# Layer norms' inverse square root: a first guess from the exponent and three Newton steps on VectorE, in place of ScalarE's root

## The chip, the core and the metric

The kernel runs on one core of a Trainium2 chip. The metric is the device time of one execution in microseconds. A core has five engines, each with its own in-order instruction queue: TensorE (PE in the profile: matrix products), VectorE (DVE: elementwise work and reductions), ScalarE (ACT: functions from tables, copies), GpSimd (POOL: here mostly the issue of gathers) and SyncE (SP: the issue of plain DMAs). An instruction that waits holds up everything behind it in its queue.

## The reference, cut to what matters

Four layers run over 4096 nodes with 128 features and one 4096 x 4096 adjacency matrix that is mostly zero. Every layer begins with the same normalisation, and the last layer has a further one inside:

```python
def _layernorm(x, axis=-1, eps=1e-5):
    m = jnp.mean(x, axis=axis, keepdims=True)
    v = jnp.var(x, axis=axis, keepdims=True)
    return (x - m) / jnp.sqrt(v + eps)

# layer 0: neigh = adj @ h; x @ W_self.T + neigh @ W_neigh.T + b
# layer 1: out = h @ w[0] + (L @ h) @ w[1] + (2 L @ (L @ h) - h) @ w[2] + b
# layer 2: attention over the entries of adj, softmax by exp(max(0.2 C, C))
# layer 3: messages gelu(s_i + d_j + b) weighted by adj, an update, gelu, a layer norm with ln_w, ln_b
for layer in (0, 1, 2, 3):
    h = jnp.maximum(_layernorm(x, axis=-1), 0.0)
    x = x + layer_ref[layer](h, adj)
```

## The kernel before

The nodes stand in 32 blocks of 128 (a block is the partition dimension), handled in 8 groups of 4 blocks. The stages are:

- The adjacency matrix is read once, row block by row block. `mark` (L763) turns each half row block into a mask with ScalarE's Sigmoid, `scan` (L774) works on the mask with VectorE, and from it come lists of the non-empty parts (`row_flags`, `col_flags`, `pairs`).
- Three propagations (`Layer.load`, `Layer.gather`, `Layer.multiply`): dense tiles near the hub nodes come by plain DMA, rows for the listed parts by gathers that GpSimd issues (L553). `begin` (L967), `finish_0` (L985), `finish_1` and `finish_2` (L1019) follow a group's sums. Meanwhile `entries` (L806) decodes single matrix entries for the last layer.
- The attention (`Attention.attend`, L1216): Relu and Exp on ScalarE (L1229, L1232), two products on VectorE (L1236, L1238), two matmuls per tile (L1253, L1255). `finish_3` (L1268) closes a stripe.
- The messages (`Messages`, L1317): `prepare` (L1355) and `message` (L1394) use Gelu (L1377, L1415), `finish` (L1428) makes the update with a Gelu (L1444), the last norm, and writes the output.

The norms are in two places. `norm` (L557) is called by `begin` for 8 blocks at a time (4 calls), and by `finish_0`, `finish_2` and `finish_3` for 4 blocks (8 calls each): 28 calls. The last norm is written out in `Messages.finish` (L1445 to L1464), 8 times. Each one goes: a sum over the features on VectorE (L563, L1448) and its scaling to minus the mean (L564, L1449); one Square with a running sum per block on ScalarE (L568, L1453); the root on ScalarE (L572, L1456); the reciprocal on VectorE (L574, L1458) and minus mean times it (L575, L1459); then one Relu or Identity per block on ScalarE with the two as scale and bias (L578, L1462).

The order of the instructions on each engine isn't written out by hand. Every piece of work is a generator that yields what it needs next: an engine with an estimated time, a free buffer or an event. `Plan.run` (L299) simulates the engines while the program is built and gives the engine to the piece that can begin first, with ranks deciding among those that can begin within 0.3 us. A yield may carry the name of a function table; if it differs from the last one, the plan adds `TABLE = 1.3` us to ScalarE's time (L340). Plain matmuls on zeros fill gaps of TensorE (`fill`, L604). `in_order` (L348) then fixes the order found. So an edit to the estimates, or to the list of steps, changes the order everywhere after it.

If a capacity of the lists was exceeded, a dense version of the stack runs (`dense_stack`); with this data it doesn't run. It keeps its own norms.

Of the kernel before, what the change touches and what calls it, by code (L numbers as in the profile page):

```python
# [18 lines left out]
I32 = mybir.dt.int32  # L19
AF = mybir.ActivationFunctionType  # L20
ALU = mybir.AluOpType
# [5 lines left out]
D = 128  # L27
P = 128
# [3 lines left out]
GB = BANK // D  # L32
HALF = N // 2
QUARTER = N // 4
EPS = 1e-5
# [322 lines left out]
def on_dve(n):  # L358
    return "DVE", 0.16 + 1.05e-3 * n
# [7 lines left out]
def on_act(n, table=None):  # L367
    return ("ACT", 0.22 + 0.83e-3 * n) + ((table,) if table else ())
# [10 lines left out]
def sparse_stack(tc, x, adj, adjT, diag, w_self, w_neigh, b0, w1, b1, w2, att_src, att_dst,  # L379
# [7 lines left out]
    nc = tc.nc  # L387
    plan = Plan()
    EARLY = 7
    with ExitStack() as ctx:  # L390
# [7 lines left out]
        def kept(name, shape, dtype=F32):  # L398
            return keep.tile(list(shape), dtype, name=name, tag=name)
# [12 lines left out]
        def by_block(v, n):  # L412

            return v[:, None, :].to_broadcast([P, n, D])
# [31 lines left out]
        nc.gpsimd.memset(ones, 1.0)  # L446
        ones8 = kept("ones8", (P, 1), F8)
        nc.gpsimd.memset(ones8, 1.0)
        eps = kept("eps", (P, 1))
        nc.gpsimd.memset(eps, EPS)  # L450

        def iota(name, shape, pattern, base=0, step=0, dtype=F32):
            t = kept(name, shape, dtype)
# [100 lines left out]
                                         in_offset=bass.IndirectOffsetOnAxis(ap=index, axis=0))  # L554


        def norm(blocks, dst):  # L557

            n = blocks.stop - blocks.start
            st = yield stats  # L560
            src = xN[:, blocks, :]
            yield on_dve(n * D)
            nc.vector.tensor_reduce(st[:, 0, :n], src, axis=AX.X, op=ALU.add)  # L563
            nc.vector.tensor_scalar_mul(st[:, 0, :n], st[:, 0, :n], -1.0 / D)  # L564
            junk = yield junks
            yield "ACT", 0.58 * n
            for k in range(n):
                nc.scalar.activation(junk, src[:, k, :], AF.Square, bias=st[:, 0, k:k + 1],  # L568
                                     accum_out=st[:, 1, k:k + 1])
            plan.release(junks, junk)  # L570
            yield on_act(n, "sqrt")
            nc.scalar.activation(st[:, 1, :n], st[:, 1, :n], AF.Sqrt, bias=eps, scale=1.0 / D)  # L572
            yield "DVE", 0.35
            nc.vector.reciprocal(st[:, 2, :n], st[:, 1, :n])  # L574
            nc.vector.tensor_mul(st[:, 3, :n], st[:, 0, :n], st[:, 2, :n])  # L575
            yield "ACT", 0.45 * n
            for k in range(n):
                nc.scalar.activation(dst[:, k, :], src[:, k, :], AF.Relu, scale=st[:, 2, k:k + 1],  # L578
                                     bias=st[:, 3, k:k + 1])
            plan.release(stats, st)  # L580
# [12 lines left out]
        def times(p, n, terms):  # L593

            for k in range(n):
                for i, (lhs, w) in enumerate(terms):
                    nc.tensor.matmul(p[:, k * D:(k + 1) * D], lhs[:, k * P:(k + 1) * P], w, start=i == 0,  # L597
                                     stop=i == len(terms) - 1)
# [13 lines left out]
        def rows_of(p, n=GB):  # L612
            return p[:, :n * D].rearrange("p (k d) -> p k d", d=D)
# [353 lines left out]
        def begin(g):  # L967
            yield x_here[g]
            yield x_here[g + 1]
            blocks = slice(g * GB, (g + 2) * GB)  # L970
            yield from norm(blocks, hA[:, blocks, :])
            for k in range(2):
                h_done[g + k].set(plan.finish)
            yield SP
            nc.sync.dma_start(rows_in(h_tabs[0])[:, blocks, :], hA[:, blocks, :])
            landed = plan.transfer(2 * P * BANK * 4)
            for k in range(2):
                h0_table.set(landed)
            yield "POOL", 2.5
            nc.gpsimd.tensor_add(xN[:, blocks, :], xN[:, blocks, :], by_block(b0_sb, 2 * GB))  # L980
            for k in range(2):
                blocks = slice((g + k) * GB, (g + k + 1) * GB)
                yield from to_features(blocks, hA[:, blocks, :])

        def finish_0(g, agg):  # L985
            blocks = slice(g * GB, (g + 1) * GB)
            rows = xN[:, blocks, :]
            p = yield banks
            yield "PE", 8 * 0.42
            times(p, GB, [(hT[:, g * BANK:(g + 1) * BANK], w_self_sb), (agg, w_neigh_sb)])  # L990
            plan.release(aggs, agg)
            yield on_dve(BANK)
            nc.vector.tensor_add(rows, rows, rows_of(p))
            plan.release(banks, p)
            yield from norm(blocks, hB[:, blocks, :D])
            h1_done[g].set(plan.finish)
            yield SP
            nc.sync.dma_start(rows_in(h_tabs[1])[:, blocks, :], hB[:, blocks, :D])
            h1_table.set(plan.transfer(P * BANK * 4))
            yield "POOL", 1.4  # L1000
            nc.gpsimd.tensor_add(rows, rows, by_block(b1_sb, GB))
            yield from to_features(blocks, hB[:, blocks, :D])
# [16 lines left out]
        def finish_2(g, agg):  # L1019
# [9 lines left out]
            plan.release(banks, p)  # L1029
            h = yield h2s  # L1030
            yield from norm(blocks, h)
            yield from to_features(blocks, h)
            plan.release(h2s, h)
# [283 lines left out]
        class Messages:  # L1317
# [110 lines left out]
            def finish(self, g):  # L1428
                blocks = slice(g * GB, (g + 1) * GB)
                plan.release(s_tiles, self.s_rows[g])  # L1430
                agg = yield aggs
                yield on_act(BANK)
                nc.scalar.copy(agg, self.acc[g])
                plan.release(accs if g else picks, self.acc[g])
                p = yield banks
                yield "PE", 8 * 0.42
                times(p, GB, [(hT[:, g * BANK:(g + 1) * BANK], upd_h_sb), (agg, upd_a_sb)])
                plan.release(aggs, agg)
                f = yield f_tiles
                yield on_dve(BANK)  # L1440
                nc.vector.tensor_tensor(f, rows_of(p), by_block(upd_b_sb, GB), op=ALU.add)
                plan.release(banks, p)
                yield on_act(BANK, "gelu")
                nc.scalar.activation(f, f, AF.Gelu)  # L1444
                st = yield stats  # L1445
                yield "DVE", 1.5
                nc.vector.tensor_add(f, f, hA[:, blocks, :])
                nc.vector.tensor_reduce(st[:, 0, :GB], f, axis=AX.X, op=ALU.add)  # L1448
                nc.vector.tensor_scalar_mul(st[:, 0, :GB], st[:, 0, :GB], -1.0 / D)  # L1449
                junk = yield junks  # L1450
                yield "ACT", 0.58 * GB
                for k in range(GB):
                    nc.scalar.activation(junk, f[:, k, :], AF.Square, bias=st[:, 0, k:k + 1], accum_out=st[:, 1, k:k + 1])  # L1453
                plan.release(junks, junk)
                yield on_act(GB, "sqrt")
                nc.scalar.activation(st[:, 1, :GB], st[:, 1, :GB], AF.Sqrt, bias=eps, scale=1.0 / D)  # L1456
                yield "DVE", 0.35
                nc.vector.reciprocal(st[:, 2, :GB], st[:, 1, :GB])  # L1458
                nc.vector.tensor_mul(st[:, 3, :GB], st[:, 0, :GB], st[:, 2, :GB])  # L1459
                yield "ACT", 0.45 * GB  # L1460
                for k in range(GB):
                    nc.scalar.activation(f[:, k, :], f[:, k, :], AF.Identity, scale=st[:, 2, k:k + 1],  # L1462
                                         bias=st[:, 3, k:k + 1])
                plan.release(stats, st)  # L1464
                yield "DVE", 1.4
                nc.vector.tensor_mul(f, f, by_block(ln_w_sb, GB))
                nc.vector.tensor_add(f, f, xN[:, blocks, :])
                yield SP
                nc.sync.dma_start(out_rows[:, blocks, :], f)
                plan.release(f_tiles, f, plan.transfer(P * BANK * 4) - 1)  # L1470
                self.through.set(plan.finish)
# [115 lines left out]
        for i in range(2):  # L1587
# [6 lines left out]
            n = max(sum(u.cap for u in g.units) for g in GROUPS)  # L1594
# [67 lines left out]
def gnn_stack_kernel(tc, **args):  # L1662


    some_bad = sparse_stack(tc, **args)
    with tc.If(some_bad > 0):
        args.pop("diag")
        dense_stack(tc, **args)
# [329 lines left out]
```

## Time and profile before

| | us |
|---|---|
| median of 3 runs | 1176.93 |
| lowest and highest | 1172.99, 1178.95 |
| the profiled execution, its own time | 1485.49 |
| its span, first to last instruction | 1483.4 |

The profiled execution is 308.56 us longer than the median. The profile's rows of single instructions are the durations in that execution. TensorE's mean granted clock in it was 0.842 of full speed.

| engine | busy us | share of the span | instructions |
|---|---|---|---|
| PE | 1055.1 | 71% | 5943 |
| DVE | 792.7 | 53% | 2982 |
| ACT | 671.2 | 45% | 1344 |
| POOL | 766.4 | 52% | 832 |

A busy share is a mean over stages that differ: the reading of the matrix ends at about 340 us, the first three layers at about 900, the attention at about 1190, and the messages fill the rest. ScalarE's ACT_TABLE_LOAD rows are the changes of its function table; the row's line is that of the function that needed the new table.

### The profile page before, as it was taken

The page shows a single profiled execution, that of the slowest core. Times are in us where ns is not written, and L with a number is a line of the kernel's source. Part 1 is how long each engine was busy: PE and PEld are TensorE (multiplying, and loading weights), DVE is VectorE, ACT ScalarE, POOL GpSimd, SP SyncE. Part 2 cuts the span into 40 slices and gives each one's busy share as a digit, 9 for nine tenths or more (in the row PEclk, how much of TensorE's full clock was granted, in tenths as well). Part 3 has the DMA queues.
Part 4 walks back from the last instruction along what each step waited for, and adds up shares of the span by engine and source line. Part 5 has one row for each costly group of instructions (what it writes and reads, how often), then busy time and mean ns, then how long its engine had stood idle before and what let it go on. Part 6 is the DMA issues. An engine that isn't in the chain of part 4 may idle for free.

```text
span 1483.4 us, 19188 instructions
## 1 busy us (share of the span) xinstructions
PE 1055.1 (71%) x5943; PEld 722.2 (49%) x5943; DVE 792.7 (53%) x2982; ACT 671.2 (45%) x1344; POOL 766.4 (52%) x832
## 2 busy tenths in 40 slices
PE   6786778877486687667677069968767872957774
PEld 2454556554265465455555045534434452645663
DVE  5796567787466476345645048444444451424453
ACT  5983466664021213113335048656555630334366
POOL 4136664344635565546656733765557346664530
PEclk9897799897697899778888579979888995988988
DMA  8999899895565777766544034333333212112210
GB/s 252 357 329 334 286 299 330 305 353 185 135 185 147 211 228 227 201 187 181 150 115 132 8 93 132 107 88 89 88 107 97 61 50 49 42 42 53 61 45 24
DMA packets 175415, 236.03 MB, mean 159 GB/s; under 512 B 22452, under 2 KB 155336, under 8 KB 167112
## 3 DMA queue, kind: packets, MB, share of 16 engines
q1 hardware_dynamic: 148904, 186.45, 37.8%
q0 software_dynamic: 26400, 48.27, 13.6%
q8 instruction: 49, 0.80, 0.2%
q14 instruction: 62, 0.51, 0.1%
HBM read 203.41 MB, written 31.23 MB: 158 GB/s over the span
## 4 chain that ended last, share of the span: by engine, by line
PE 23%; another core or an unknown queue 13%; ACT 10%; DVE 7%; issue 6%; DMA 1%; POOL 0%; ACTq 0%; SPq 0%; DVEq 0%; POOLq 0%
PE acc L1253 4%; PE acc L1255 3%; PE bank L597 2%; PE acc L1421 2%; PE acc L1139 2%; PE acc L1156 2%; ACT junk L1453 1%; ACT e L1229 1%; ACT junk L568 1%; PE bank L1411 1%; PE pick L610 1%; ACT e L1232 1%; PE bank L1409 1%; DVE ehit L891 1%
## 5 line engine op out<-in xcount | busy, mean ns | idle before, releaser
L553 POOL DMA_INDIRECT e_val<-in_adj,e_at x158 | 154.5, 978 | 48.0 <-issue 45.6
L553 POOL DMA_INDIRECT g<-h_tab,fetch_row x136 | 136.1, 1001 | 73.0 <-issue 34.3
L610 PE MATMUL pick<-nothing 128*128 128x512 f16 x536 | 142.9, 416 | 1.6 <-issue 1.6
L1139 PE MATMUL acc<-big,hA 128*128 128x256 f32 x448 | 131.7, 442 | 10.7 <-issue 7.7
L610 PEld LDWEIGHTS <-nothing 128*128 128x128 f16 x795 | 82.9, 107 | 99.3 <-issue 33.4
L553 POOL DMA_INDIRECT g<-a_tab,fetch_col x74 | 76.9, 1039 | 93.6 <-issue 45.3
L553 POOL DMA_INDIRECT rseg<-in_adjT,seg_row x68 | 71.1, 1046 | 103.4 <-issue 28.8
L1139 PEld LDWEIGHTS acc<-big,hA 128*128 128x128 f32 x448 | 96.4, 225 | 28.6 <-issue 9.5
L553 POOL DMA_INDIRECT cseg<-in_adj,seg_col x74 | 70.8, 957 | 63.9 <-issue 23.2
L891 DVE SCALAR_TENSOR_TENSOR ehit<-ehit,pos,pick 128x32 f32<-128x32 f32 (+7 forms) x158 | 38.8, 285 | 116.0 <-issue 80.1
L1236 DVE TENSOR_TENSOR tau<-e,big 128x512 f32<-128x512 f32 (+3 forms) x61 | 54.3, 891 | 85.5 <-ACT e L1232 47.8
L553 POOL DMA_INDIRECT g<-u_tab,fetch_row x68 | 64.6, 950 | 64.9 <-PE acc L1156 37.1
L888 ACT COPY ehit<-pick 128x192 f32<-128x192 f32 (+7 forms) x74 | 20.4, 286 | 154.5 <-remote 80.4
L553 POOL DMA_INDIRECT tau<-d_tab,e_col x63 | 60.6, 962 | 57.2 <-issue 15.0
L769 ACT ACTIVATE mask<-dst 128x2048 fp8e4<-128x2048 f32 x43 | 81.8, 1903 | 14.2 <-DMA dst<-in_adj 8.0
L553 POOL DMA_INDIRECT m<-d_tab,e_col x70 | 68.4, 977 | 38.5 <-issue 17.4
L1156 PE MATMUL acc<-big,g 128*128 128x256 f32 x272 | 80.2, 434 | 0.6 <-DMA big<-r_tab 0.5
L568 ACT ACTIVATE junk<-xN,stat 128x128 f32<-128x128 f32 x128 | 51.4, 401 | 60.0 <-DVE stat L564 27.0
L623 ACT ACTIVATE sel_t<-iota_row,mids 128x512 f32<-128x512 f32 (+3 forms) x43 | 27.1, 642 | 109.7 <-DVE mids L618 63.7
L610 PE MATMUL bank<-nothing 128*128 128x512 f16 x259 | 70.6, 414 | 2.7 <-issue 2.3
L884 PE MATMUL pick<-eA,esel 128*128 128x65 f16 (+7 forms) x158 | 27.0, 245 | 61.4 <-DVE esel L625 28.0
L1139 PE MATMUL acc<-big,hB 128*128 128x256 f32 x224 | 62.7, 420 | 1.7 <-DMA big<-in_adjT 1.7
(331 smaller groups left out, 2717.2 us busy)
## 6 DMA issues: line engine op xcount, KB each, us to landing
dst<-in_adj SPq DMA_DIRECT2D x43, 1024.0 KB
big<-in_adjT SPq DMA_DIRECT2D x45, 512.0 KB
raw<-in_adj SPq DMA_DIRECT2D x21, 1024.0 KB
big<-in_adjT SPq DMA_DIRECT2D x66, 256.0 KB
big<-r_tab SPq DMA_DIRECT2D x30, 512.0 KB
c_tab<-cseg SPq DMA_DIRECT2D x74, 128.0 KB
r_tab<-rseg SPq DMA_DIRECT2D x68, 128.0 KB
big<-c_tab SPq DMA_DIRECT2D x15, 512.0 KB
```

Source lines behind the costliest of these rows:

```text
L553: nc.gpsimd.indirect_dma_start(out=dst, out_offset=None, in_=table[:, :], in_offset=bass.IndirectOffsetOnAxis(ap=index, axis=0))
L568: nc.scalar.activation(junk, src[:, k, :], AF.Square, bias=st[:, 0, k:k + 1], accum_out=st[:, 1, k:k + 1])
L597: nc.tensor.matmul(p[:, k * D:(k + 1) * D], lhs[:, k * P:(k + 1) * P], w, start=i == 0, stop=i == len(terms) - 1)
L610: nc.tensor.matmul(idle[2][idle[1]], nothing[:, :P], nothing, start=True, stop=True)
L769: nc.scalar.activation(mask[:, h * HALF:(h + 1) * HALF], raw_of[b, h], AF.Sigmoid, scale=1e38, accum_out=marks[:, 2 * b + h:2 * b + h + 1] ...
L891: nc.vector.scalar_tensor_tensor(hit[:, q, :], hit[:, q, :], pos0[:, k + q:k + q + 1], pv[:, q, W:2 * W], op0=ALU.is_le, op1=ALU.mult, acc ...
L1139: nc.tensor.matmul(acc, self.near[:, b, :D], as_rows(t)[:, k, :], start=count == 0, stop=count == every - 1)
L1156: nc.tensor.matmul(acc, row[:, :D], r, start=count == 0, stop=count == every - 1)
L1236: nc.vector.tensor_mul(tau[:, :n, :], e[:, :n, :], a[:, :n, :])
L1253: nc.tensor.matmul(acc[0:1, CS:2 * CS], parts[k][:, D + 1:], tau[:, k, :], start=False, stop=False)
L1255: nc.tensor.matmul(acc[:, :CS], parts[k][:, :D], e[:, k, :], start=False, stop=self.count[s.index] == every - 1)
L1421: nc.tensor.matmul(acc[:, b % GB * P:(b % GB + 1) * P], m[:, q, :], r[:, q, :], start=False, stop=all(self.left[g * GB + k] == 0 for k in ...
```

## The change

The function `inverse_root` is new. It takes the sum of squared differences in `st[:, 1]`, scales it to the variance and adds EPS, takes a first guess of the inverse root by halving the number's bits and subtracting them from a constant, and makes three Newton steps, all on VectorE. Both places of a norm call it where they took the root and its reciprocal. The estimates of the plan change with it: ScalarE's step with the table name "sqrt" and VectorE's 0.35 us go, VectorE's 1.6 us come. The tile `eps` and its memset go.

```diff
-        eps = kept("eps", (P, 1))
-        nc.gpsimd.memset(eps, EPS)
...
+        def inverse_root(st, n):
+
+            v, y, t = (st[:, k, :n] for k in (1, 2, 3))
+            nc.vector.tensor_scalar(v, v, 1.0 / D, EPS, op0=ALU.mult, op1=ALU.add)
+            nc.vector.tensor_scalar(y.bitcast(I32), v.bitcast(I32), 1, None, op0=ALU.logical_shift_right)
+            nc.vector.tensor_scalar(y.bitcast(I32), y.bitcast(I32), -1.0, float(0x5f3759df), op0=ALU.mult, op1=ALU.add)
+            for _ in range(3):
+                nc.vector.scalar_tensor_tensor(t, y, -0.5, y, op0=ALU.mult, op1=ALU.mult)
+                nc.vector.tensor_mul(t, t, v)
+                nc.vector.scalar_tensor_tensor(y, t, 1.5, y, op0=ALU.add, op1=ALU.mult)
...
             plan.release(junks, junk)
-            yield on_act(n, "sqrt")
-            nc.scalar.activation(st[:, 1, :n], st[:, 1, :n], AF.Sqrt, bias=eps, scale=1.0 / D)
-            yield "DVE", 0.35
-            nc.vector.reciprocal(st[:, 2, :n], st[:, 1, :n])
+            yield "DVE", 1.6
+            inverse_root(st, n)
             nc.vector.tensor_mul(st[:, 3, :n], st[:, 0, :n], st[:, 2, :n])
...
                 plan.release(junks, junk)
-                yield on_act(GB, "sqrt")
-                nc.scalar.activation(st[:, 1, :GB], st[:, 1, :GB], AF.Sqrt, bias=eps, scale=1.0 / D)
-                yield "DVE", 0.35
-                nc.vector.reciprocal(st[:, 2, :GB], st[:, 1, :GB])
+                yield "DVE", 1.6
+                inverse_root(st, GB)
                 nc.vector.tensor_mul(st[:, 3, :GB], st[:, 0, :GB], st[:, 2, :GB])
```

## The prediction, made before the change was run

> **What bounds the kernel now.** I read the page's slices first, then the chain of waits, then the groups of ScalarE by shape, and last the timeline around a few norms.
>
> ```profile
> ACT  5983466664021213113335048656555630334366
> PEclk9897799897697899778888579979888995988988
> DMA  8999899895565777766544034333333212112210
> ```
>
> The rows are 40 slices of 37 us. To slice 9 (about 350 us) DMA is busy at 0.8 to 0.9 in most slices; afterwards nothing is full for long. The busy times by stretch say the same; their columns are the stretch, its length, busy us and instructions of PE, PEld, DVE, ACT and POOL, the clock, the DMA share and GB/s.
>
> ```profile
> 40.00:100.00 60.00, 46.09 (x387) 29.18 (x385) 52.07 (x184) 57.51 (x102) 8.72 (x5) 0.91 0.97 346
> 220.00:280.00 60.00, 49.90 (x388) 34.11 (x387) 40.21 (x105) 36.46 (x55) 27.96 (x27) 0.89 0.92 318
> ```
>
> While the matrix is read, transfers are at 0.92 to 0.97, whatever ScalarE does (57.5 us of 60, then 36.5 of 60). So the reading is bound by transfers, with ScalarE and VectorE close behind in one stretch.
>
> ```profile
> PE 23%; another core or an unknown queue 13%; ACT 10%; DVE 7%; issue 6%; DMA 1%; POOL 0%; ACTq 0%; SPq 0%; DVEq 0%; POOLq 0%
> ```
>
> This is the chain that ended last, by engine. Its pieces begin at 579 us; of the time before, the reading among it, it says nothing. "Another core or an unknown queue" is mostly engines standing still beside a running queue of gathers: 13% is about 198 us, with pieces of 27 and 32 us. With "issue", 6%, that is some 290 us, nearly the 308.56 us by which the profiled execution (1485.49 us) exceeds the median (1176.93 us). I take these stalls to be largely the profiled execution's, and the work between them to be common to both. ScalarE has 10% of the chain. What of that is table changes?
>
> ```profile
> L572 ACT ACT_TABLE_LOAD x26 | 33.4, 1283 | 0.5
> L769 ACT ACT_TABLE_LOAD x10 | 12.8, 1283 | 0.2
> L1232 ACT ACT_TABLE_LOAD x8 | 10.3, 1283 | 0.1
> L1456 ACT ACT_TABLE_LOAD x8 | 10.3, 1283 | 0.1
> L1042 ACT ACT_TABLE_LOAD x7 | 9.0, 1283 | 0.1
> L1377 ACT ACT_TABLE_LOAD x6 | 7.7, 1283 | 0.1
> ```
>
> Columns: busy us and mean ns, then the idle time before. With one each at L1482 and L1444 and three at L1415 there are 70 changes of the table, 89.8 us of ScalarE's 671.2. L572 and L1456 are the roots (34 changes); the others mostly change back.
>
> ```profile
> 1328.36 0.19 ACT L1453 ACTIVATION_READ_ACCUMULATOR junk<-f,stat 128x1 f32 x1
> 1328.56 1.28 ACT L1456 ACT_TABLE_LOAD   x1
> 1329.86 0.30 ACT L1456 ACTIVATE stat<-stat,eps 128x4 f32<-128x4 f32 x1
> 1330.17 1.28 ACT L1377 ACT_TABLE_LOAD   x1
> 1330.19 0.18 DVE L1458 RECIPROCAL stat<-stat 128x4 f32<-128x4 f32 x1 [3.16 <-ACT stat L1456]
> 1330.40 0.16 DVE L1459 TENSOR_TENSOR stat<-stat 128x4 f32<-128x4 f32 x1
> 1331.47 0.63 ACT L1377 ACTIVATE own<-own 128x512 f32<-128x512 f32 x1
> 1332.00 1.63 ACT L1462 ACTIVATE f<-f,stat 128x128 f32<-128x128 f32 x4
> ```
>
> One norm of the messages. The Squares end, the table is changed for the root, the root takes 0.30 us, and the table is changed back for a Gelu before the Identity: 1328.56 to 1332.00, 3.44 us. VectorE's part hides under the second change.
>
> **What the Trainium skill says.** "ScalarE: Activation LUTs", section "Table sets", says that sqrt, sigmoid, exp and gelu anchor different sets, and that cheap functions lie in every set. The trace agrees: Square (L568), Relu (L578) and Copy (L590) never have a change. Section "What ACT_TABLE_LOAD costs" gives 1283 ns and about 1380 ns of drain. The trace shows 1283 ns and no drain (1328.56 to the root's start at 1329.86), so I count 1.28. "VectorE: DVE Perf Modes", section "The DRAIN you can't avoid", says to minimise the count of chained operations, since each waits for the pipe to empty. In this trace that holds for dependent ones:
>
> ```profile
> 155.43 0.17 DVE L670 TENSOR_SCALAR pnone<-at_block 128x5 f32<-128x5 f32 x1
> 155.63 0.17 DVE L671 TENSOR_TENSOR prow<-prow,pnone 128x5 f32<-128x5 f32 x1
> 155.83 0.17 DVE L672 CAST fetch_row<-prow 128x5 uint32<-128x5 f32 x1
> 156.03 0.42 DVE L673 TENSOR_SCALAR prow<-prow 128x5 f32<-128x5 f32 x1
> ```
>
> Each begins 0.20 us after the one it depends on, though it takes 0.17.
>
> **The change, part by part.** *ScalarE.* 36 roots of 0.30 us go, 10.7 us. All 34 changes to the root's table go. Of the other 36, those that changed back go too. What is left is the first, sigmoid, exp, and gelu with a return to exp where a group's messages are prepared inside the attention (997 us), and gelu for the rest: about 6. So 64 x 1.28 = 82 us, with the roots 93 us of ScalarE, lie somewhere; the chain says where.
>
> *VectorE.* Each norm gets 3 + 3 x 3 = 12 operations on 4 or 8 columns in place of one reciprocal, each needing the one before: 12 x 0.20 = 2.40 us for 0.20, so 36 x 2.2 = 79 us more, 872 us in all against a span of 1483.4. No row shows the shift of float bits or these shapes of the fused product. The nearest rows give 0.16 to 0.18 (L575 0.163, L564 0.175, L644 0.175, integer L904 of seven columns 0.165), so 0.16 below (no dependence) and 0.25 above a step; I keep 0.20. Port sharing with the gathers isn't seen and not charged.
>
> *One norm's latency.* The last norm (1472.41) has nothing beside it: change 1.28, root 0.30, reciprocal and product, 2.05 us from the last Square to the Identity. After: 2.40 + 0.20 and two hand-overs of 0.03, 2.66. So a bare norm is 0.61 slower. A norm with a function behind it, like the one shown, goes from 3.44 to 2.66, 0.8 faster. If the plan finds other work for ScalarE in the gap, the gain is all of 1.28 + 0.30 + 1.28 = 2.86. The plan is told 1.6 us for what takes 2.6, so it may put the Relu or Identity up to 1.0 us too early; what stands behind it on ScalarE is copies that free banks for TensorE, the attention's Relu and Exp, and message Gelus that TensorE's L1421 waits for. That is why 2.86 won't be had everywhere.
>
> *Layer 2 (596 to 900 us).* On the chain: four changes at L1042 and part of one, 5.3 us, two roots with changes, 3.2, and 0.97 of a change at L1232: 9.5. Two bare norms give back 1.2, and each last store of a table, which the next gathers wait for on SP and POOL, is 0.6 later. Between 2 and 9.5, I take 5.
>
> *Attention (900 to 1198).* Five roots, 5 x 1.59 = 8.0, the change being charged to "issue" in four, and six changes back at L1232, 7.6: 15.6. If only the norms' own gaps shrink, 5 x 0.8 = 4. There is other ScalarE work here (180 us busy of the 290), so fill is likely: I take 10.
>
> *Messages (to the end).* Eight roots with changes, 12.7, and seven changes back at L1377, L1415 and L1444, 9.0: 21.7 on the chain. All filled it is 7 x 2.86 - 0.61 = 19.4; with gaps alone 7 x 0.8 - 0.61 = 5. Fill depends on gathers having landed, so 11.
>
> *Reading and layers 0 and 1 (to 596).* Twenty changes and 12 roots leave ScalarE, 29 us; 12 x 2.2 = 26 us come to VectorE, where the matrix's scan waits behind them (52 of 60 us busy from 40 to 100). Transfers hide both; if that cover is gone it is -10 to +8. I take -2.
>
> *VectorE later on.* 24 x 2.2 = 53 us more on an in-order engine that is half idle; behind a Newton chain stand the evacuations of banks and the attention's products. 0 to -10, I take -3. The eps memset and tile: nothing, POOL has it before 20 us. No DMA is added or taken away; the plan will move many past each other, which I can't price (a few us, either sign).
>
> Sum: 5 + 10 + 11 - 2 - 3 = 21 us. 1485.49 becomes 1464.5. Since the durations are of instructions that aren't stretched (every change is 1283 ns), I carry the 21 us over whole: 1176.93 - 21 = 1156.
>
> **The rivals.** (1) *Filled entirely:* the plan packs ScalarE; 9.5 + 15.6 + 19.4 = 44.5 go, 1132. For it: the plan charges 1.3 us for each change and now has none to arrange. Against it: 2.6 us for 1.6. (2) *Hidden anyway:* the gathers are the bound. POOL issues them one in 1.25 us, and the chain's standing parts follow them; only the low ends count, 2 + 4 + 5 less 2 + 3, so 6 or less, about 1173. Against it: the chain of the last 130 us runs through Squares, changes and Identities of ScalarE. (3) *VectorE becomes the path, slower:* the Newton chain is an unbroken 2.4 us at a high rank, in front of the scan in the reading and of evacuations later. It decides if over about a third of the added 79 us is felt: 26 against the 11 of the low ends, 15 slower, 1192. For it: VectorE's 52 of 60 us in the early stretch, and that TensorE's banks wait for VectorE; against it: about 690 us in which VectorE is idle. That the changes of the table stay is hardly possible, since no function of another set stands between.
>
> **How the numbers follow.** Forecast 0.55 (1143 to 1168); rival 1 0.14; rival 2 0.17; rival 3 0.14. Half a per cent, 5.9 us, is about what a measurement of this kernel tells from no change. Rival 2 splits into 0.05 faster, 0.10 same, 0.02 slower. So faster 0.55 + 0.14 + 0.05 = 0.74, same 0.10, slower 0.16. The bounds of all terms together give 52 us faster to 9 slower, 1125 to 1186; leaving out a tenth at each side, 1136 to 1184.
>
> **What would show it.** About 6 table changes in place of 70, ScalarE's busy time near 580 us, VectorE's near 870. Twelve operations 0.20 us apart between the last Square and L575's product. In the messages, from the last Square to the Identity about 2.7 us, with other Gelus in it where the forecast holds and an idle ScalarE where rival 2 does. If VectorE appears in the chain with far more than its 7%, or the reading stage ends later than 340 us, rival 3 is right. I am wrong in the main step if the table changes are gone and the attention and messages last as long as before.

## The result, and the profile after

| | before | after |
|---|---|---|
| median of 20 runs | 1177.15 us | 1177.50 us |
| lowest and highest | 1168.60, 1183.77 | 1169.62, 1180.19 |
| ratio, 95% interval | | 0.9999 [0.9982, 1.0015] |

The change makes no difference that can be measured; the forecast was 21 us faster. Chips come in two conditions here, whatever the kernel: the two sets of 20 runs and the profile after are from one (about 1177 us), the profile before (1485.49 us) and runs e1 to e16 below, on four chips, from the other (medians of 1480 to 1515 us for the kernel before), so all ratios below are to the kernel before on the same chip.

The page of the kernel after, its busy times, then slices of 29 us:

```profile
PE 969.8 (83%) x5852; PEld 666.7 (57%) x5852; DVE 860.3 (73%) x3378; ACT 582.6 (50%) x1244; POOL 774.0 (66%) x831
...
DVE  6799988879888777667888865666567672356683
ACT  4885556656523222232434457477678641244563
POOL 5127746536446777767777777777777777777770
PEclk9989989878989989888989999989989999999998
DMA  7999999999857888889866653443445222222321
...
PE 16%; POOL 8%; DMA 8%; DVE 8%; issue 6%; ACT 4%; POOLq 0%; ACTq 0%; DVEq 0%
```

The last line is the chain that ended last. "Another core or an unknown queue" had 13% before and is gone; ScalarE has 4% in place of 10%. POOL stands at 7 from about 380 us to the end: gathers one behind the other. VectorE is at 7 to 9 from the second slice to the tenth and has 73% of the span. In the profile before it had 792.7 us, which were 53% because that span is 308 us longer; of 1177 us they are 67%. The stretches that the prediction showed, with the same columns, after:

```profile
40.00:100.00 60.00, 46.30 (x381) 30.04 (x380) 52.60 (x185) 48.24 (x91) 19.05 (x15) 0.91 1.00 362
220.00:280.00 60.00, 50.84 (x407) 33.07 (x406) 52.90 (x147) 34.64 (x47) 26.73 (x27) 0.79 0.97 333
```

ScalarE lost 9 us of 57.5 in the first; in the second VectorE went from 40.2 to 52.9 of 60. These two profiles are from different conditions, so this isn't the change alone.

What the change was to do on ScalarE, it did. All the table changes of the kernel after, by line:

```profile
L1487 ACT ACT_TABLE_LOAD x1 | 1.3, 1283 | 0.7 <-PEq L1991 0.7
L776 ACT ACT_TABLE_LOAD x1 | 1.3, 1283 | 0.0
L1049 ACT ACT_TABLE_LOAD x1 | 1.3, 1283 | 0.0
L1384 ACT ACT_TABLE_LOAD x1 | 1.3, 1283 | 0.0
L1239 ACT ACT_TABLE_LOAD x1 | 1.3, 1283 | 0.0
L1422 ACT ACT_TABLE_LOAD x1 | 1.3, 1283 | 0.0
```

Six for 70. Now one norm of the messages. The timeline of ScalarE in the kernel after (start, us, what):

```profile
1105.77 0.19 ACT L1460 ACTIVATION_READ_ACCUMULATOR junk<-f,stat 128x1 f32 x1
1105.86 0.61 ACT L1384 ACTIVATE own<-own 128x512 f32<-128x512 f32 x1
1106.38 0.85 ACT L1422 ACTIVATE m<-bank 128x384 f32<-128x384 f32 x2
1108.75 1.65 ACT L1467 ACTIVATE f<-f,stat 128x128 f32<-128x128 f32 x4 [1.52 <-DVE stat L1464]
```

The timeline of VectorE in the same stretch:

```profile
1105.99 0.35 DVE L558 TENSOR_SCALAR stat<-stat 128x4 f32<-128x4 f32 x1 [1.71 <-ACT junk L1460]
1106.38 0.17 DVE L559 TENSOR_SCALAR stat<-stat 128x4 int32<-128x4 int32 x1
1106.58 0.17 DVE L560 TENSOR_SCALAR stat<-stat 128x4 int32<-128x4 int32 x1
1106.79 0.16 DVE L562 SCALAR_TENSOR_TENSOR stat<-stat 128x4 f32<-128x4 f32 x1
1106.98 0.16 DVE L563 TENSOR_TENSOR stat<-stat 128x4 f32<-128x4 f32 x1
1107.18 0.16 DVE L564 SCALAR_TENSOR_TENSOR stat<-stat 128x4 f32<-128x4 f32 x1
...
1108.55 0.16 DVE L1464 TENSOR_TENSOR stat<-stat 128x4 f32<-128x4 f32 x1
1108.63 0.87 DVE L1388 TENSOR_SCALAR r<-ident,diag_sb 128x128 f32<-128x128 f32 x4
```

From the last Square to the Identity it is 2.79 us (1105.96 to 1108.75); it was 3.44. The plan has put Gelus of 1.4 us into the gap, and ScalarE stands for 1.52 more (the bracket: idle before, and what ended it). Over all 36 norms this standing is the idle time of four groups; columns: busy us and mean ns, idle us before and what ended it.

```profile
L585 ACT ACTIVATE hA<-xN,stat 128x128 f32<-128x128 f32 x64 | 25.8, 480 | 6.8 <-DVE stat L582 6.8
L585 ACT ACTIVATE hB<-xN,stat 128x128 f32<-128x128 f32 x32 | 13.2, 482 | 13.1 <-DVE stat L582 13.1
L585 ACT ACTIVATE h<-xN,stat 128x128 f32<-128x128 f32 x32 | 13.2, 482 | 21.1 <-DVE stat L582 21.1
L1467 ACT ACTIVATE f<-f,stat 128x128 f32<-128x128 f32 x32 | 13.2, 482 | 11.4 <-DVE stat L1464 11.4
```

52.4 us; before it was 4.3, most of it in one group:

```profile
L578 ACT ACTIVATE h<-xN,stat 128x128 f32<-128x128 f32 x32 | 13.2, 482 | 3.6 <-DVE stat L575 3.2 <-issue 0.4
```

About half of the 93 us that ScalarE was freed of have come back as standing (51.6 us in e5, on a chip in the other condition). That looked like the cause. The experiments say that it is not the main one.

### The profile page after: what moved, and what is told of

It reads as the page before. It is cut to its first block, busy times and chain, and to the rows that moved or that the text cites. A ratio compares the mean times of both kernels' runs of the same rounds, so it can differ in the third digit from the quotient of the medians.

```text
span 1175.2 us, 19297 instructions
## 1 busy us (share of the span) xinstructions
PE 969.8 (83%) x5852; PEld 666.7 (57%) x5852; DVE 860.3 (73%) x3378; ACT 582.6 (50%) x1244; POOL 774.0 (66%) x831
## 4 chain that ended last, share of the span: by engine, by line
PE 16%; POOL 8%; DMA 8%; DVE 8%; issue 6%; ACT 4%; POOLq 0%; ACTq 0%; DVEq 0%
POOL e_val L551 5%; PE acc L1262 3%; PE acc L1260 3%; DMA tau<-d_tab,e_col 2%; DMA m<-d_tab,e_col 2%; DMA g<-a_tab,fetch_col 2%; POOL g L551 1%; PE bank L604 1%; PE acc L1428 1%; DMA e_val<-in_adj,e_at 1%; PE bank L1416 1%; PE bank L1418 1%; ACT junk L1460 1%; POOL m L551 1%; ACT e L1236 1%
## 5 line engine op out<-in xcount | busy, mean ns | idle before, releaser
L551 POOL DMA_INDIRECT e_val<-in_adj,e_at x158 | 160.4, 1015 | 48.0 <-issue 41.0
L1146 PE MATMUL acc<-big,hA 128*128 128x256 f32 x448 | 117.5, 404 | 1.3 <-DMA big<-in_adjT 1.3
L617 PE MATMUL pick<-nothing 128*128 128x512 f16 x439 | 115.9, 410 | 0.0
L617 PEld LDWEIGHTS <-nothing 128*128 128x128 f16 x704 | 71.3, 104 | 78.4 <-issue 18.4
L551 POOL DMA_INDIRECT m<-d_tab,e_col x79 | 77.7, 983 | 24.1 <-issue 14.6
L1146 PEld LDWEIGHTS acc<-big,hA 128*128 128x128 f32 x448 | 85.9, 202 | 12.4 <-DMA big<-in_adjT 1.7
L1163 PE MATMUL acc<-big,g 128*128 128x256 f32 x272 | 76.3, 411 | 11.7 <-DMA big<-r_tab 7.8
L551 POOL DMA_INDIRECT tau<-d_tab,e_col x67 | 66.3, 989 | 20.4 <-issue 11.0
L1163 PEld LDWEIGHTS acc<-big,g 128*128 128x128 f32 x272 | 51.4, 202 | 23.6 <-issue 8.4
L1163 PE MATMUL acc<-rseg,g 128*128 128x256 f32 x136 | 47.6, 455 | 15.2 <-DMA g<-h_tab,fetch_row 15.1
```

The source lines that it names most:

```text
L551: nc.gpsimd.indirect_dma_start(out=dst, out_offset=None, in_=table[:, :], in_offset=bass.IndirectOffsetOnAxis(ap=index, axis=0))
L617: nc.tensor.matmul(idle[2][idle[1]], nothing[:, :P], nothing, start=True, stop=True)
L1146: nc.tensor.matmul(acc, self.near[:, b, :D], as_rows(t)[:, k, :], start=count == 0, stop=count == every - 1)
L1163: nc.tensor.matmul(acc, row[:, :D], r, start=count == 0, stop=count == every - 1)
```

## The experiments

Ratios are to the kernel before on the same chip, with 95% intervals. The letters in the expectations are those of the theories that they state. Three questions were asked: are the gathers the bound, so that it doesn't matter what the norms do; what are the change's parts worth, each alone; and how do the Newton steps cost what they cost.

### Are the gathers the bound?

**e1**: the kernel before, run once more. 1473.83 us.

> The kernel before once more, for a profile in the same condition as that of the changed kernel. Theory G (the queue of gathers on GpSimd sets the end after the matrix is read): POOL's digits stand at 0.7 from about 380 us to the end, as in the changed kernel, with gathers 1.25 us apart, and the chain of waits runs through gathers; the span is within 1% of 1177. Theory V (the table changes were on the path and VectorE's Newton steps took their place): the chain holds at least 20 us of table changes and roots, and in the changed kernel about as much of L558 to L564.

The profile was like the one before, not within 1% of 1177: POOL's digits mostly at 4 to 7, no continuous gathers. So the long time of the profile before wasn't an accident of one execution.

**e5**: the kernel after, on such a chip. Without it no experiment there could be held against the result.

> The changed kernel itself, beside the kernel before on this chip. The last runs had the kernel before at 1484 us where the comparison had 1177, with about 290 us of standing waits in the profile. Where the kernel before is at about 1177: ratio 0.998 to 1.002, as measured. Where it is at about 1484: theory G (gathers alone) says 0.995 to 1.005. Theory S (there the engines' semaphores are answered late while gathers are issued one after the other, so each dependent operation costs more than 0.20 us) adds the two parts up, 0.998 for the table changes and 1.035 for the Newton steps, 1.02 to 1.04.

1.0048 [1.0018, 1.0078]: no gain in this condition either, rather 7 us lost.

**e4** and **e12**: a short memset of GpSimd behind every gather, in the kernel after and in the one before.

```diff
+        spare = kept("spare", (P, P))
         def gather(dst, table, index):
             nc.gpsimd.indirect_dma_start(out=dst, out_offset=None, in_=table[:, :],
                                          in_offset=bass.IndirectOffsetOnAxis(ap=index, axis=0))
+            nc.gpsimd.memset(spare, 0.0)
```

> The changed kernel with one memset of 128x128 on GpSimd behind every gather (0.20 us by the row L446), order and plan as they are. About 610 of 738 gathers come after 340 us. Theory G: up to 610 x 0.20 = 122 us longer, and at least half of that if the memset fits partly into the 0.30 us that GpSimd stands between two gathers: ratio 1.05 to 1.10. Theory V: GpSimd has slack, under 1.01.

> The kernel before with the memset of 128x128 on GpSimd behind every gather, as e4 had it in the changed kernel (ratio 0.971). Theory S (gathers one after the other hold up the other engines, and spacing them helps): 0.965 to 0.98 here too. If e4's gain belongs to the changed kernel alone, 0.995 or above. Against e4 it also says what the change is worth with the gathers spaced: if the standing alone hid the gain, e4 is 5 to 20 us below this one.

0.9706 [0.9637, 0.9775] and 0.9714 [0.9659, 0.9768]. GpSimd's 736 memsets of 0.23 us make the kernel 3% *faster*, with either norm. For e4 that is a miss of sign by the theory of the gathers (G); e12, expected after it, came out as said. Gathers in a row begin 1.33 us apart here, in place of 1.25. So in this condition the rate at which GpSimd issues isn't what bounds the kernel, and spacing does the same with root and with Newton steps. In the condition of the result, where POOL stands at 7 to the end, it wasn't tried.

**e6** and **e7**: the kernels before and after without the 158 gathers of single matrix values (`e_val`), which are left out with 1.0 in their place.

```diff
-        nc.gpsimd.memset(e_val, 0.0)
+        nc.gpsimd.memset(e_val, 1.0)
...
-                        yield GATHER
-                        n = u.within(k)
-                        gather(e_val[:n, k:k + 1], adj_flat, e_at[:n, k:k + 1])
```

> The kernel before without the 158 gathers of single matrix values; 1.0 stands in their place, so the weights of the messages are left out. This takes 158 x 1.25 = 197 us from GpSimd's queue. Theory G: well over half of it shows, 100 to 170 us faster (ratio 0.86 to 0.92). Theory V (GpSimd has slack, table changes and Newton steps cancel): under 40 us, 0.97 or above.

> The changed kernel without the same 158 gathers, 1.0 in their place. Theory G: as much faster as the one before; and if the gathers alone hid the gain, the changed kernel is now 5 to 20 us faster than the kernel before without them. If the two stay within 5 us, something else besides the gathers hides or cancels it. Theory V: under 40 us.

0.8992 [0.8933, 0.9052] and 0.8957 [0.8911, 0.9002]: 10% go, 150 us, as theory G had it for e6 (V had under 40). The kernel after is now the faster by 8.7 us of medians, which is inside G's 5 to 20, but the intervals overlap. So the gathers do cost much of the time, and this pair doesn't rule out that they cover a part of the gain. That they alone hid it is ruled out, for this condition, by the runs that follow: there each part of the change moves the time with all gathers in place.

### The parts alone

**e2** and **e9**: the root replaced by an Identity of the same shape, so that nothing changes the table (the root is left out). In e2 the plan is told so and makes another order; e9 keeps the first line of the diff, and with it the order of the kernel before. The last norm is edited likewise, here and below.

```diff
-            yield on_act(n, "sqrt")
-            nc.scalar.activation(st[:, 1, :n], st[:, 1, :n], AF.Sqrt, bias=eps, scale=1.0 / D)
+            yield on_act(n)
+            nc.scalar.activation(st[:, 1, :n], st[:, 1, :n], AF.Identity, bias=eps, scale=1.0 / D)
```

> The kernel before with Identity in place of the root, so that the root is left out and some 64 table changes with it; VectorE keeps its one reciprocal. ScalarE gets about 82 us lighter and VectorE no heavier. Theory G: no change, ratio 0.995 to 1.005. Theory V: the whole gain of my forecast shows, 1177 - 21 - 5 (no VectorE cost), about 1151, ratio 0.978.

> The kernel before in its own order, with Identity in place of the root: the root is left out and its table changes are gone, and nothing else is different. It shows what the table changes cost by themselves, without a new order. Theory H (they are hidden, whatever the order): ratio 0.995 to 1.003. Theory C (they cost what my sum said, and something gives it back): 21 to 26 us faster, ratio 0.982 to 0.986.

e2 0.9979 [0.9944, 1.0014], as G had it; e9 0.9894 [0.9841, 0.9947], between its two theories. The 64 changes of the table are worth 1.06%, 16 us of 1480 (8 to 24 by the interval), if the order stays; with the order that the plan makes without them, 3 us.

**e3** and **e10**: root and table changes kept, and the twelve Newton operations on VectorE on top. e3 tells the plan (1.95 us); e10 keeps the 0.35 and so the old order.

```diff
-            nc.scalar.activation(st[:, 1, :n], st[:, 1, :n], AF.Sqrt, bias=eps, scale=1.0 / D)
-            yield "DVE", 0.35
-            nc.vector.reciprocal(st[:, 2, :n], st[:, 1, :n])
+            nc.scalar.activation(st[:, 3, :n], st[:, 1, :n], AF.Sqrt, bias=eps, scale=1.0 / D)
+            yield "DVE", 1.95
+            nc.vector.reciprocal(st[:, 2, :n], st[:, 3, :n])
+            inverse_root(st, n)
```

> The kernel before with its roots, reciprocals and table changes, and the 12 Newton operations on top in every norm: 36 x 2.4 = 86 us more on VectorE, nothing taken from ScalarE. Theory G: no change, ratio 0.995 to 1.008. Theory V: 20 us slower or more, since the Newton steps cost what the table changes gave, ratio 1.017 or above.

> The kernel before in its own order, roots and table changes kept, the 12 Newton operations on top. It shows what VectorE's 86 us cost by themselves. The Newton instructions in the old order were 1.5% slower with the table changes gone (e8). Theory C: the sum of both effects is +22 us, so +40 us here, ratio 1.025 to 1.035. Theory H: table changes give nothing, so the same as e8, ratio 1.010 to 1.020.

1.0355 [1.0299, 1.0410] and 1.0254 [1.0185, 1.0323]. In the old order 432 operations more on VectorE, 86 us at 0.20 each, cost 37.6 us of 1480 (27 to 48).

**e8**: the instructions of the kernel after in the order of the one before. **e11**: the instructions before in the order of the one after. Only the plan's estimates are exchanged, and with the order the plan lays 5943 matmuls in e8 and 5852 in e11, a difference of 91 fillers on zeros; the diff is e8's, and e11's is its reverse.

```diff
-            yield "DVE", 1.6
+            yield on_act(n, "sqrt")
+            yield "DVE", 0.35
```

> The changed kernel's instructions in the order that the plan made for the kernel before: the plan still counts the root with its table change and 0.35 us of VectorE. Theory O (the new order gave a gain back): 10 to 20 us faster than the changed kernel. Theory G: within 6 us of it.

> The root, its table changes and the reciprocal, in the order that the plan made for the changed kernel. Order alone. If the new order is worth the 15 us or more that lie between e8 and the changed kernel whatever the instructions, this is 0.985 to 0.992 of the kernel before. If the new order is only good with the table changes gone (ScalarE's queue is filled by it), it is slower: 1.005 to 1.03.

1.0148 [1.0082, 1.0214] and 1.0147 [1.0099, 1.0194]. e8 is slower than the kernel after, where both of its theories had it faster or level. In the old order the change loses 22 us of 1484, which is the sum of the two parts measured alone: -16 + 38 = +22. The order that the plan makes for it takes it from 1.0148 to 1.0048 (e5), some 15 us; for the root the same order is 22 us worse than its own. So in this condition three terms nearly cancel, and none of them is nothing. The difference of e8 and e9, Newton steps against an Identity and a reciprocal in one order, is 2.5% again, as in e10.

### How the Newton steps cost 38 us

Two ways were open: ScalarE's Relu or Identity waits behind a chain that takes longer than the plan believes, or the chain holds up whatever else stands behind it on VectorE.

**e14**: the kernel before, root and all, and the twelve operations on a spare tile *behind* the product that the Relu needs.

```diff
...
             nc.vector.tensor_mul(st[:, 3, :n], st[:, 0, :n], st[:, 2, :n])
+            inverse_root(spare, n)
...
```

> The kernel before in its own order, with the root and the table changes; the twelve Newton operations run on a spare tile behind the product of each norm, so that nothing on ScalarE waits for them. W: at most 1.008. O: 1.02 to 1.026, as with the twelve operations ahead of the product (1.0254).

1.0257 [1.0197, 1.0317], against e10's 1.0254. Two of the groups of ScalarE's outputs in e10:

```profile
L590 ACT ACTIVATE hA<-xN,stat 128x128 f32<-128x128 f32 x64 | 25.9, 482 | 11.9 <-DVE stat L587 8.1 <-DVE stat L566 3.4 <-issue 0.4
...
L590 ACT ACTIVATE h<-xN,stat 128x128 f32<-128x128 f32 x32 | 13.2, 482 | 24.1 <-DVE stat L587 19.4 <-DVE stat L566 4.8
```

The same two in e14:

```profile
L593 ACT ACTIVATE hA<-xN,stat 128x128 f32<-128x128 f32 x64 | 26.0, 485 | 1.7 <-DVE stat L589 1.6
...
L593 ACT ACTIVATE h<-xN,stat 128x128 f32<-128x128 f32 x32 | 13.2, 486 | 2.0 <-DVE stat L589 1.4 <-issue 0.4
```

With the other two groups, standing is 51.6 us in e10 and 4.1 in e14, and the cost is the same as far as the intervals tell (a difference of about 13 us either way would not show). So ScalarE's wait isn't the main cost; what the two runs share is that VectorE is occupied. It doesn't work by stretching the gathers: one takes GpSimd 0.99 us in e9 and in e10 and 0.98 in e14.

Who waits for VectorE is seen only in part. TensorE's weight loads wait for it 187 us in all in e10, 208 in e14 and 184 in e8, and 149 in e9 and 174 and 144 in two profiles of the kernel before. One of these waits: engine, line, what is waited for, us in total, times, longest. In the kernel before and in e9:

```profile
PEld L884 <- DVE esel L625: 33.5, 14, 6.6
```
```profile
PEld L884 <- DVE esel L625: 26.1, 8, 7.5
```

In e10, e14 and e8:

```profile
PEld L896 <- DVE esel L637: 50.0, 10, 18.0
```
```profile
PEld L899 <- DVE esel L640: 48.8, 9, 15.0
```
```profile
PEld L892 <- DVE esel L633: 19.9, 7, 8.8
```

In e10 and e14 TensorE waits longer for the selection of matrix entries (`esel`, made by VectorE). In e8, with the same twelve operations, it doesn't, so this is one place and not the cause by itself. When it happens is plainer: e8's gathers start within 9 us of e9's up to 690 us, then 10 us later at 731, 26 at 975, 37 at 1233, where two profiles of the kernel before differ by up to 10 us; e10's are 9 us behind e9's at 387 and 36 at 947. Most of the time is lost after the reading, which ends at about 340 us.

**e13**: the kernel after, the plan told 2.8 us for the chain and the product in place of 1.6.

> The changed kernel with the plan told 2.8 us, about what the Newton chain with its product takes, in place of 1.6 in both norms. Theory W (the Newton steps cost time because ScalarE's Relu or Identity is put behind a chain that the plan takes for 1.6 us): the standing of ScalarE before the norms' outputs falls from 51.5 us below 30, and the time from 1.0048 of the kernel before to 0.985 to 0.995. Theory O (they cost time because twelve operations hold up what stands behind them on VectorE): the standing may fall, the time stays within 0.7% of 1.0048, by the luck of the order.

On this chip the kernel before scattered from 1494 to 1542 us, and no interval was to be had: medians 1498.5 against 1515.1, 0.989. The standing stayed at 54.5 us. Telling the plan the true time doesn't take the wait away; whether the order it makes gains 1% is open.

**e15** and **e18**: two Newton steps in place of three, so a less exact root, the plan told 2.1. **e17**: two steps, without the second part of the diff, the plan still told 1.6, so that the order is that of the kernel after and only 108 operations are fewer.

```diff
-            for _ in range(3):
+            for _ in range(2):
...
-            yield "DVE", 1.6
+            yield "DVE", 2.1
```

> The changed kernel with two Newton steps in place of three (nine operations, 1.8 us by 0.20 each), the plan told 2.1. Both theories: a quarter of the 38 us goes, about 10, so 0.995 to 1.0 of the kernel before; W adds the part that the truer 2.1 gives back, so below 0.995.

> The two steps told 2.1 once more, on another chip if it comes so, since the kernel before scattered by 3% beside the first (1494 to 1542). 0.97 to 0.98 if the first result holds, 0.985 to 1.0 if it was the scatter; what it has below the two steps in the old order's place is the order that 2.1 makes.

> The changed kernel with two Newton steps, the plan told 1.6 us as for three, so that the order of every engine is that of the changed kernel and three operations of each norm are gone, 108 in all. If time goes with the operations: 12 of 48, a quarter of the 38 us, about 10, so 0.995 to 1.0 of the kernel before (three steps: 1.0048). If the 0.9735 of the two steps told 2.1 came from operations alone: 0.97 to 0.98.

e15 0.9735 [0.9648, 0.9822], on the scattering chip, below all that was expected. e17 and e18 then came on a chip in the condition of the result (before 1178.26 us): e17 1167.87 us, 0.9916 [0.9886, 0.9946], and e18 1172.26, 0.9957 [0.9933, 0.9980]. The first 0.9735 didn't hold there. e17 against the result's 0.9999, in one order, is the operations alone: 0.83%, 9.8 us (6 to 14 by the two intervals), for 108 operations that take 21.6 us at 0.20 each: 45% felt, where e10 had 38 of 86, 44%. A quarter of the operations thus costs more than the prediction charged for all of them. Its page beside that of the kernel after:

```profile
PE 973.3 (83%) x5852; PEld 670.1 (57%) x5852; DVE 839.2 (72%) x3270; ACT 582.5 (50%) x1244; POOL 770.0 (66%) x831
```

Same counts on every engine but VectorE, 3270 for 3378. The gathers start within 3 us of those of the kernel after up to 420 us, and 4 us earlier at 730, 6 at 975 and 8.4 at the last one: here the time goes after the reading, which ends at 319 us. So the operations cost about as much in the condition of the result as in the other. That it is by occupying VectorE there too isn't shown, since the chain is shorter as well and ScalarE's standing fell from 52.4 us to 34.7.

**e16**: two steps told 2.1, and the memset behind every gather.

> The same with a memset of GpSimd behind every gather. If the spacing of the gathers acts apart from the norms as in the two runs that had it (about 3% each), 0.963 to 0.968; above 0.971 the two steps are worth nothing beside it.

0.9560 [0.9492, 0.9628], below what was expected, against e15's 0.9735 on the same chip: spacing adds 1.8% there. Whether the two together would beat e17 in the faster condition wasn't tried. In the condition of the result both e17 and e18 are below the kernel before, e17 the further; the kernel after was not run on their chip.

## Why the prediction was wrong, point by point

- **What happens to instructions: right.** About 6 table changes (6), ScalarE near 580 us (582.6), VectorE near 870 (860.3), twelve operations 0.20 us apart (the chain's median is 2.42 us to the product, predicted 2.40), 2.7 us from Square to Identity (2.79).
- **"5 + 10 + 11" for the table changes: too large.** e9 measured 16 us (8 to 24) for 26. The chain of waits showed 47 us of changes and roots on it, and the prediction took about half; a third was there.
- **"VectorE later on ... 0 to -10, I take -3", and "-2" for the reading: the step that failed.** Together 5 us; e10 and e14 measured 38, and e17 alone 9.8 for a quarter of the operations in the condition of the result. The argument was that VectorE is half idle. The 53% was read over a span with some 300 us of stalls that the prediction itself set aside; of 1177 us it is 67%. And a mean doesn't say what the added operations delay. It was mostly not the reading, where VectorE's 52 of 60 us were shown: the gathers fall behind after it. There TensorE waits for particular products of VectorE, whatever the mean.
- **Rival 3, VectorE becomes the path: right on that cost.** It put the point of decision at a third of the added time felt; 44% was, and in the old order the change does lose time, 22 us (e8), where the rival said 15. Its sign, VectorE with far more than 7% of the chain of waits, didn't come (8%). That share is no measure of the cost: it is 25% in e10 and 4% in e14, which lose about the same.
- **The rest of a norm's latency: right in kind, wrong in weight.** The prediction feared the plan's 1.6 us for what takes 2.6, and ScalarE did stand, 52.4 us in all. e14 loses as much without that standing.
- **"The plan will move many past each other, which I can't price (a few us, either sign)": undersized.** The order alone moved the time by +1.5% (e11 against the kernel before), -1.0% (e5 against e8) and +0.9% (e2 against e9), each pair with the same instructions except for 91 to 109 of TensorE's fillers, which the plan lays with the order and which weren't tried apart: as much as the terms that were priced. That it gave back 15 us here is luck; the same order costs the kernel with the root 22.
- **Stalls "largely the profiled execution's": wrong.** They go with the chip. On four chips every execution of the kernel before took 1463 to 1542 us, and e1's profile has the same stalls. Carrying the 21 us over whole did little harm: the net is +7 us in that condition and zero in the other.
- **Rival 2, hidden anyway, 1173 us**, came nearest in time and for the wrong reason: where the parts were measured, a gain and a loss cancelled.

In us of the slower condition, the sum was -26 + 5 = -21; the runs give -16 + 38 - 15 = +7. For the result's own condition only the net (0.9999) and the price of VectorE's operations (e17) were measured, not the parts -16 and -15.

The Trainium skill, "VectorE: DVE Perf Modes", says in its section "The DRAIN you can't avoid" that the next operation doesn't start until the pipe is empty. The advice to minimise the count of operations, which the prediction quoted from there, stands in the same page's section "Rules for kernel authors"; it was the advice to weigh most. The trace after agrees for dependent operations, 0.20 us from start to start where one takes 0.16, but the next one on VectorE (L1388), which doesn't need the one ahead of it, starts 0.08 us after that one. e17 puts a price on the count for a whole kernel, 0.09 us (9.8 / 108) for each operation taken away.

## What to carry to other kernels

A mean share of 53% doesn't make an engine free: price added operations by the stretches in which others wait for that engine, and if that isn't known, keep half of their time as a loss in the range (44% and 45% were felt here). Where a planner orders the instructions, run the new instructions in the old order and the old ones in the new, before judging the instructions; the order is a term of its own. And when a change moves nothing, measure its halves alone: no effect and two cancelling effects look alike in the total, and only the second leaves something to gain (here one Newton step fewer).

## What the runs showed of the hardware that was not expected

One program takes 1177 us on some chips and 1480 to 1515 on others. In the slower ones over 200 us of the span have no work on TensorE, VectorE or ScalarE at all (218.5 in the profile before, 206.8 in e1, 240.6 in e5, with TensorE's weight loads counted as work); in the profile after, 34.7. TensorE's mean granted clock, for the kernel before, was 0.82 to 0.85 on these chips and 0.92 to 0.94 on the one of e17. In the profile before, 161 us without work fall into rows of three or more gathers one behind another, which fill 61% of the span; the rest falls elsewhere. The timeline of ScalarE in the profile before, at such a place:

```profile
828.10 0.17 ACT L1042 ACTIVATE hB<-bank 128x2 f32<-128x2 f32 x1 [15.11 <-remote]
855.43 0.24 ACT L888 COPY ehit<-pick 128x96 f32<-128x96 f32 x1 [27.16 <-remote]
```

VectorE there:

```profile
828.38 0.41 DVE L1045 TENSOR_TENSOR hB<-bank,hB 128x256 f32<-128x256 f32 x1
855.71 0.25 DVE L891 SCALAR_TENSOR_TENSOR ehit<-ehit,pos,pick 128x32 f32<-128x32 f32 x1 [26.91 <-issue]
```

And GpSimd:

```profile
828.83 0.94 POOL L553 DMA_INDIRECT e_val<-in_adj,e_at  x1 [0.30 <-issue]
...
853.79 0.94 POOL L553 DMA_INDIRECT e_val<-in_adj,e_at  x1 [0.30 <-issue]
855.04 0.93 POOL L553 DMA_INDIRECT e_val<-in_adj,e_at  x1 [0.30 <-issue]
```

Both engines stand for 27 us, for nothing that the profile shows, and go on just before the row of gathers ends. A memset of 0.23 us behind each gather (e12) leaves 159.8 us without work and takes 3% off the time. In the profile after, 315 gathers stand in one row, and the engines go on beside them. That gathers in a row hold the other engines on the slower chips is suggested by this and not shown, and why it would be so on these chips alone isn't known.
